# A four-layer graph network, layer 3: split repeat tiles in PSUM, a longer closing pipeline, ten gather sets

## The chip, the cores and the metric

The kernel runs on one core of one Trainium2 chip. The metric is the device time of one execution in microseconds (us); several runs are given by their median. In the profile the engines are PE (TensorE: matmul; PEld is its weight load), DVE (VectorE), ACT (ScalarE), POOL (GpSimd, which here issues the indirect DMAs) and SP (SyncE, which issues plain DMAs).

## The reference

Four layers over 2708 nodes with 128 features. Each is followed by a residual addition and a layer norm. The adjacency matrix is sparse (about 16 neighbours in a row), and the kernel works on lists of neighbours. The change is in the last layer, a graph attention with four heads:

```python
def _gatv2_head(x, A_shape, w1, w2, a, Wlin):
    x1 = x @ w1
    x2 = x @ w2
    E = jax.nn.leaky_relu(x1[:, None, :] + x2[None, :, :], negative_slope=0.01)
    s = E @ a
    s = jnp.tanh(s / 8.0) * 8.0
    s = jnp.exp(s) * A_shape
    s = s / jnp.sum(s, axis=-1, keepdims=True)
    out = s @ x @ Wlin.T
    return jax.nn.leaky_relu(out, negative_slope=0.01)
...
heads = [_gatv2_head(x, A_shape, w1[h], w2[h], a[h], Wlin[h]) for h in range(w1.shape[0])]
return jnp.concatenate(heads, axis=-1) @ w
...
x = _layernorm(x + _L3_gnn_ref(x, adj, ...), axis=-1)
```

## The kernel before

Layer 3 sorts the nodes by their number of neighbours into 24 blocks (`BLOCKS3`, a pair each: neighbour slots g of a node, and quads j of the block, 3 to 8). A chunk is up to 128 edges, one to a partition. Four chunks make a quad; there are 100 quads. `quads` lists them in order, and the loop from L1541 on runs over them.

For each quad the engines do this:

- `fetch` (L1530) takes a tile `g4` of 4 chunks x 644 numbers from the pool `got` and fills it with four indirect DMAs on POOL (L247). A row is x2 of the neighbour for four heads (512), its x (128) and four linear score terms. The pool has `GOT` such sets; a set comes free when the last matmul that reads it is done. `fetch` is called one quad ahead, but POOL runs further ahead as far as sets are free.
- `repeated` (L1350) repeats the block's own x1 over the edges: four matmuls with 32 rows of contraction each (L1358). Three go into the tile `z3` (three PSUM banks), the fourth into `z1`, and a matmul with the identity (L1363) adds the fourth chunk of `g4` to `z1`.
- DVE adds `z3` to the first three chunks (L1555, one instruction over 1536 numbers), scores the fourth out of PSUM (`scores`, L1373, four instructions), and multiplies the relu of the others by the attention vector (`products`, L1381).
- ACT sums these products for each head (`sums_of_products`, L1389: 12 sums in an even quad, 8 in an odd one, where DVE scores the third chunk itself).

Two quads are closed together in `rest` (L1394), a Python generator that hands on at each `yield`. Its stages before: (1) DVE adds the linear terms, L1400 and L1403; (2) ACT tanh and exp, L1405 and L1406; (3) DVE times the adjacency value `val3`, L1409; (4) PE sums over a node's edges, L1414, into `few_ps`; (5) DVE reciprocal `inv` L1419, product L1420, and the mask that spreads the weights into `wm`, L1422; (6) PE multiplies `wm` with x of the neighbours into `po_s`, L1435, which reads the `g4` set for the last time.

When a block's last pair is through, `finish` (L1443) follows: ACT copies `po_s` to `o_ts` (L1448), PE multiplies by Wlin into `pl_s` (L1456), ACT and DVE make the leaky relu `lin_s` (L1461, L1463), PE multiplies by w (L1469 and L1475, into `few_ps`), ACT copies to `y_s` (L1480). After several blocks `normalised3` does the layer norm and scatters the rows out on POOL (L255).

`own_terms` (L1311) prepares the next block while a block's first quads run: a transpose into `few_ps` (L1316), ACT's copy `x_ot` (L1319), x1 and its linear term on PE (L1323 into its own bank, L1324 into `few_ps`), ACT's copy of x1 (L1327) and `al` on DVE (L1330), a matmul into `few_ps` (L1339), and a copy on ACT (L1345).

The order on PE, DVE and ACT is the order in which this Python code calls the instructions. `step` (L1514) advances the generators one stage: the first of `finishing`, then up to two of `closing`, then one of `preparing`. It is called three times in each quad: after the adds and scores (before `repeated` of the next quad), after `products`, and after the sums. I call the three steps of an even quad A, B, C and those of the odd quad behind it D, E, F. A pair's `rest` enters `closing` after its step F, so before the change its six stages fall on A to F of the next pair. A block with an odd number of quads closes its last quad alone, and its `rest` starts in the middle of such a row of steps.

`few_ps` is one PSUM bank, shared by the sums of L1414 (two places), the transpose, the own terms and the output of L1475.

Of the kernel before, what the change touches and what calls it, by code (L numbers as in the profile page):

```python
# [9 lines left out]
FP = mybir.dt.float32  # L10
AF = mybir.ActivationFunctionType
ALU = mybir.AluOpType
# [3 lines left out]
P = 128  # L16
# [5 lines left out]
HEADS = 4  # L22
# [7 lines left out]
HD = HEADS * D  # L30
# [48 lines left out]


TOGETHER3 = [(0, 4), (4, 8), (8, 12), (12, 16), (16, 20), (20, 23), (23, 24)]
GOT = 9


@with_exitstack
def gnn_resnorm_kernel(
# [21 lines left out]
    nc = tc.nc  # L108
# [228 lines left out]
    with ExitStack() as layer:  # L337
        ring = layer.enter_context(tc.tile_pool(name="ring", bufs=RING))
        work = layer.enter_context(tc.tile_pool(name="work", bufs=1))
        small = layer.enter_context(tc.tile_pool(name="small", bufs=2))  # L340
# [692 lines left out]
        ahead = own_row(0)  # L1033
        left = list(range(SPLIT, NBLK))
        for i, b in enumerate(TURNS):
            if i == SPLIT - 2:
                sorted_lists(1)
            x_s, ahead = ahead, own_row(TURNS[i + 1]) if i + 1 < NBLK else None
# [7 lines left out]
            for _ in range(2 if i < 1 else 1):  # L1046
                if left:
                    e = left.pop(0)
# [15 lines left out]
            for _ in range(2 if i in (9, 10, 11) else 1):  # L1064
                if i and again:
                    e = again.pop(0)
# [31 lines left out]
    with ExitStack() as layer:  # L1098
        work = layer.enter_context(tc.tile_pool(name="bn", bufs=1))
        small = layer.enter_context(tc.tile_pool(name="bn_small", bufs=2))  # L1100
# [138 lines left out]
    with ExitStack() as layer:  # L1239
        work = layer.enter_context(tc.tile_pool(name="s3", bufs=1))  # L1240
        mine = layer.enter_context(tc.tile_pool(name="s3_mine", bufs=2))
        got = layer.enter_context(tc.tile_pool(name="s3_got", bufs=GOT))
        small = layer.enter_context(tc.tile_pool(name="s3_small", bufs=3))
        ps_z = layer.enter_context(tc.tile_pool(name="s3_ps_z", bufs=1, space=PSUM))
# [52 lines left out]
        own, closing, finishing, preparing, wide, sums_of = {}, [], [], [], [], {}  # L1297
# [52 lines left out]
        def repeated(b, j, g4):  # L1350

            g, _ = BLOCKS3[b]
            e = g * (P // g)
            z3 = ps_z.tile([P, 3, HD], FP, name="z3")
            z1 = ps_z.tile([P, HD], FP, name="z1")
            for r in range(4):
                rows = slice(32 * r, 32 * r + 32)
                nc.tensor.matmul(  # L1358
                    z3[0:e, r, :] if r < 3 else z1[0:e],
                    lhsT=copies[g][rows, j, :], rhs=own[b][1][rows, :],  # L1360
                    start=True, stop=r < 3, skip_group_check=r == 3,
                )
            nc.tensor.matmul(  # L1363
                z1[0:e], lhsT=ident[0:e, 0:e], rhs=g4[0:e, 3, 0:HD],
                start=False, stop=True, skip_group_check=True,
            )
            return z3, z1

        def scores(e, r, z, a, g4, sc):

# [23 lines left out]
        def rest(b, js, g4s, sc):  # L1394

            g, jj = BLOCKS3[b]
            x_o, _, al = own[b]
            e, k = g * (P // g), 4 * len(js)
            s = sc[0:e, 0:k, :]
            nc.vector.tensor_tensor(s, s, al[0:e, 4 * js[0] : 4 * js[0] + k, :], ALU.add)  # L1400
            for i in range(len(js)):
                s4 = sc[0:e, 4 * i : 4 * i + 4, :]
                nc.vector.tensor_tensor(s4, s4, g4s[i][0:e, :, HD + D : RW], ALU.add)  # L1403
            yield
            nc.scalar.activation(s, s, AF.Tanh, scale=0.125)  # L1405
            nc.scalar.activation(s, s, AF.Exp, scale=8.0)  # L1406
            yield
            c0 = CHUNK3[b] + 4 * js[0]
            nc.vector.tensor_tensor(  # L1409
                s, s, val3[0:e, c0 : c0 + k].unsqueeze(2).to_broadcast((e, k, HEADS)), ALU.mult  # L1410
            )
            yield
            pd = pds[js[0] // 2 % 2]
            nc.tensor.matmul(  # L1414
                pd[0:e, 0:k, :], lhsT=same[g][0:e, :], rhs=s, start=True, stop=True
            )
            yield
            inv = small.tile([P, 8, HEADS], FP, name="inv")
            nc.vector.reciprocal(inv[0:e, 0:k, :], pd[0:e, 0:k, :])  # L1419
            nc.vector.tensor_tensor(s, s, inv[0:e, 0:k, :], ALU.mult)  # L1420
            wm = small.tile([P, 8, g, HEADS], FP, name=f"wm{g}", tag="wm")
            nc.vector.tensor_tensor(  # L1422
                wm[0:e, 0:k],
                mask[g][0:e].unsqueeze(1).unsqueeze(3).to_broadcast((e, k, g, HEADS)),
                s.unsqueeze(2).to_broadcast((e, k, g, HEADS)),
                ALU.mult,
            )
            yield
            if js[0] == 0:
                sums_of[b] = ps_o.tile([P, 512], FP, name="po_s")  # L1430
            po = sums_of[b]
            for i, j in enumerate(js):
                for r in range(4):
                    p0 = 32 * r + j * g
                    nc.tensor.matmul(  # L1435
                        po[:, p0 * HEADS : (p0 + g) * HEADS],
                        lhsT=g4s[i][0:e, r, HD : HD + D], rhs=wm[0:e, 4 * i + r, :, :],
                        start=True, stop=True,
                    )
            if js[-1] == jj - 1:  # L1440
                finishing.append(finish(b, po, x_o))
# [70 lines left out]


        def step(early=True):  # L1514
            for queue, most in ((finishing, 1), (closing, 2), (preparing, 1)):
                if queue is not preparing or early:
                    for work_of in list(queue[:most]):
                        if next(work_of, "done") == "done":
                            queue.remove(work_of)
# [8 lines left out]
        gathered = {}  # L1528
# [9 lines left out]

        fetch(0)
        ahead = repeated(*quads[0], gathered[0])  # L1540
        for i, (b, j) in enumerate(quads):  # L1541
            g, jj = BLOCKS3[b]
            e = g * (P // g)
            if j == 0:
                if b + 1 < NB3:
                    preparing.append(prepare(b + 1))
            if j % 2 == 0:
                sc, g4s = small.tile([P, 8, HEADS], FP, name="sc_s", bufs=4), []
            g4, (z3, z1) = gathered.pop(i), ahead
            g4s.append(g4)  # L1550
            sc4 = sc[:, 4 * (j % 2) : 4 * (j % 2) + 4, :]
            if i + 1 < len(quads):
                fetch(i + 1)
            z = g4[0:e, 0:3, 0:HD]
            nc.vector.tensor_tensor(z, z, z3[0:e], ALU.add)  # L1555
            scores(e, 3, z1, a_99.rearrange("p h d -> p (h d)"), g4, sc4[:, 3, :])
            step()
            if i + 1 < len(quads):
                while quads[i + 1][0] not in own or len(own[quads[i + 1][0]]) < 3:
                    step()  # L1560
                ahead = repeated(*quads[i + 1], gathered[i + 1])
            count = 2 if j % 2 else 3
            products(e, g4, count)
            step()
            sums_of_products(e, g4, sc4, count)
            if count == 2:
                scores(e, 2, g4[:, 2, 0:HD], a_ps, g4, sc4[:, 2, :])
            step()
            if j % 2 or j == jj - 1:
                closing.append(rest(b, list(range(j - j % 2, j + 1)), g4s, sc))  # L1570
# [526 lines left out]
```

## Time and profile before

| | us |
|---|---|
| median of 3 runs | 1935.91 (1930.33 to 1936.26) |
| the profiled execution | 1938.44 |
| its span, first to last instruction | 1936.7 |
| mean granted clock of PE | 0.667 of full speed |
| first and last add L1555 of layer 3 | 1124.99 and 1895.48 |

Busy over the whole span, by engine: PE 1240.9, DVE 1166.6, ACT 776.5, POOL 892.8 us. The groups of layer 3 that matter here, from the list of the costliest groups: busy time, then mean of one in ns.

| line, engine, what | count | us, ns each |
|---|---|---|
| L1358 PE z, four repeats of a quad | 800 | 221.3, 944 (four run side by side) |
| L1363 PE z, identity | 200 | 169.3, 941 |
| L1435 PE po_s | 800 | 128.6, 316 |
| L1555 DVE add of three chunks | 100 | 175.0, 1750 |
| L1381 DVE products | 100 | 151.0, 1510 |
| L1373 DVE scores out of PSUM | 400 | 91.9, 285 |
| L1389 ACT sums | 1024 | 301.3, 296 |
| L247 POOL gather of g | 400 | 398.6, 996 |

A matmul in fp32 appears as two records, so counts on PE are twice those in the code. A row "A <- B: 32.2, 13, 4.0" in the view of waits says that A sat idle 32.2 us in all, 13 times, at most 4.0 us, until B ended; where the releaser is "remote" or "issue", the profile shows none. The releaser is inferred. In the view of windows each engine's busy time is followed by its number of instructions.

### The profile page before, as it was taken

The numbers are of one execution on the slowest core, as the hardware profiler recorded it, in microseconds if no ns is written. First come the engines' busy times: TensorE is split into PE (matmuls) and PEld (weight loads), VectorE is DVE, ScalarE is ACT, GpSimd is POOL, SyncE is SP. The second block draws the span as 40 slices with busy tenths as digits, with TensorE's granted clock in tenths as the row PEclk, the third lists the DMA queues.
The fourth block names the chain that finished last, engine by engine and source line by source line (L and its number), as shares of the span: only waits on it lengthen the run. The fifth ranks groups of instructions, "written<-read, shape, count | busy, mean of one in ns | idle before, by whom it ended". The sixth has DMA issues, their size and how long they took to land. (4 is left out here: it accounts for less than half of the span.)

```text
span 1936.7 us, 23643 instructions
## 1 busy us (share of the span) xinstructions
PE 1240.9 (64%) x5771; PEld 864.1 (45%) x5771; DVE 1166.6 (60%) x4895; ACT 776.5 (40%) x3156; POOL 892.8 (46%) x1003
## 2 busy tenths in 40 slices
PE   7974313353446553554673748888788788878885
PEld 7973212242334442554663314544444444444444
DVE  8997445675635423433447417777678677676774
ACT  3565345543324210211122415555455555445553
POOL 1004654445653366445331474655555556555430
PEclk9986555555555576776676756676676777666675
DMA  8642645666545525223231574865566655756540
GB/s 283 238 150 79 131 140 165 174 183 174 141 103 142 177 43 160 95 92 140 79 113 44 167 239 131 212 190 163 145 196 183 182 166 160 191 150 192 150 115 7
DMA packets 167676, 289.63 MB, mean 150 GB/s; under 512 B 49600, under 2 KB 121502, under 8 KB 160429
## 3 DMA queue, kind: packets, MB, share of 16 engines
q0 software_dynamic: 60496, 190.77, 34.4%
q1 hardware_dynamic: 99489, 92.57, 15.6%
q10 hardware_dynamic: 7544, 4.69, 1.0%
q8 instruction: 48, 0.79, 0.2%
q14 instruction: 99, 0.81, 0.1%
HBM read 242.51 MB, written 45.36 MB: 149 GB/s over the span
## 5 line engine op out<-in xcount | busy, mean ns | idle before, releaser
L247 POOL DMA_INDIRECT g<-t_dram,idx x400 | 398.6, 996 | 316.0 <-issue 178.9
L247 POOL DMA_INDIRECT msg<-d_dram,idx x368 | 348.6, 947 | 260.2 <-issue 164.8
L1389 ACT ACTIVATE sum_junk<-g 126x128 bf16<-126x128 f32 (+3 forms) x1024 | 301.3, 296 | 142.4 <-issue 59.8
L1358 PE MATMUL z<-x,copies 32*126 32x512 f32 (+3 forms) x800 | 221.3, 944 | 65.8 <-DVE g L1555 45.0
L969 PE MATMUL pt_a<-ident,rows 128*128 128x128 f32 (+2 forms) x475 | 114.1, 395 | 144.4 <-ACT at_sb L974 79.5
L1555 DVE TENSOR_TENSOR g<-g,z 126x1536 f32<-126x1536 f32 (+3 forms) x100 | 175.0, 1750 | 44.0 <-DMA g<-t_dram,idx 15.3
L1018 PE MATMUL acc<-x_nat,at_rows 128*128 128x128 f32 (+2 forms) x968 | 160.7, 326 | 52.3 <-DMA at_rows<-at_dram,perm 26.5
L1389 ACT ACTIVATION_READ_ACCUMULATOR sum_junk<-g 126x1 f32 (+3 forms) x1024 | 191.6, 187 | 0.0
L1018 PEld LDWEIGHTS acc<-x_nat,at_rows 128*128 128x128 f32 (+2 forms) x968 | 144.1, 232 | 65.5 <-issue 38.7
L1363 PE MATMUL z<-g,ident 126*126 126x512 f32 (+3 forms) x200 | 169.3, 941 | 0.7 <-issue 0.7
L1435 PE MATMUL po_s<-wm,g 126*128 126x24 f32 (+6 forms) x800 | 128.6, 316 | 58.5 <-DVE wm L1422 56.2
L1435 PEld LDWEIGHTS po_s<-wm,g 126*128 126x128 f32 (+3 forms) x800 | 124.8, 243 | 75.6 <-DVE wm L1422 67.9
L969 PEld LDWEIGHTS pt_a<-ident,rows 128*128 128x128 f32 (+2 forms) x475 | 82.9, 205 | 167.5 <-ACT at_sb L974 92.8
L884 DVE SCALAR_TENSOR_TENSOR own<-msg,ls,own 128x128 f32<-128x128 f32 (+1 forms) x302 | 105.6, 350 | 85.4 <-ACT msg L899 28.5
L1381 DVE SCALAR_TENSOR_TENSOR g<-g,a_ps 126x1536 f32<-126x1536 f32 (+6 forms) x100 | 151.0, 1510 | 0.0
L420 PE MATMUL acc<-x_nat,rows 128*128 128x129 f32 (+3 forms) x1012 | 128.5, 288 | 26.0 <-DMA rows<-in_adj_dram 14.9
L420 PEld LDWEIGHTS acc<-x_nat,rows 128*128 128x128 f32 (+2 forms) x1012 | 123.0, 198 | 31.2 <-DMA rows<-in_adj_dram 16.0
L1358 PEld LDWEIGHTS z<-x,copies 32*126 32x126 f32 (+3 forms) x800 | 67.8, 261 | 100.3 <-issue 46.5
L899 ACT ACTIVATE msg<-msg 128x896 f32<-128x896 f32 (+4 forms) x55 | 50.4, 917 | 132.9 <-DVE msg L896 92.1
L1373 DVE SCALAR_TENSOR_TENSOR g<-z,a 126x128 f32<-126x128 f32 (+3 forms) x400 | 91.9, 285 | 19.5 <-remote 9.2
L445 DVE FIND_INDEX8 ci<-cv,rows 128x8 uint32<-128x247 f32 (+2 forms) x242 | 98.7, 408 | 0.0
L1363 PEld LDWEIGHTS z<-g,ident 126*126 126x126 f32 (+3 forms) x200 | 42.0, 263 | 124.3 <-issue 117.3
(302 smaller groups left out, 2132.2 us busy)
## 6 DMA issues: line engine op xcount, KB each, us to landing
rows<-in_adj_dram SPq DMA_DIRECT2D x34, 1354.0 KB
at_dram<-at_sb SPq DMA_DIRECT2D x105, 256.0 KB
g<-t_dram,idx POOLq DMA_INDIRECT x400
msg<-d_dram,idx POOLq DMA_INDIRECT x368
t_dram<-t_row SPq DMA_DIRECT2D x21, 256.0 KB
x_s<-dx_dram SPq DMA_DIRECT2D x21, 128.0 KB
at_dram<-at_sb SPq DMA_DIRECT2D x21, 64.0 KB
t_dram<-x_nat SPq DMA_DIRECT2D x5, 256.0 KB
```

The costliest lines, as they stand in the source:

```text
L247: nc.gpsimd.indirect_dma_start(out=dst, out_offset=None, in_=table[0:N, :], in_offset=bass.IndirectOffsetOnAxis(ap=index, axis=0),)
L420: nc.tensor.matmul(accs0[k][0:m, c0 : c0 + f1 - f0], lhsT=rows[0:n, j0 : j0 + m], rhs=x_nat[0:n, b, f0:f1], start=k not in started, stop=( ...
L445: nc.vector.max_index(out=ci[0:n, at], in_max=cv[0:n, at], in_values=rows[0:n, c0 : c0 + cw])
L884: nc.vector.scalar_tensor_tensor(to, m, v, last, ALU.mult, ALU.add)
L969: nc.tensor.transpose(pt[0:m, j, 0:n], rows[0:n, c0 : c0 + m], ident[0:n, 0:n])
L1018: nc.tensor.matmul(accs2[ib // 4][0:m, (ib % 4) * D : (ib % 4 + 1) * D], lhsT=at[0:n, i0 : i0 + m], rhs=xw[0:n, b, :], start=(k == 0 and i ...
L1358: nc.tensor.matmul(z3[0:e, r, :] if r < 3 else z1[0:e], lhsT=copies[g][rows, j, :], rhs=own[b][1][rows, :], start=True, stop=r < 3, skip_g ...
L1363: nc.tensor.matmul(z1[0:e], lhsT=ident[0:e, 0:e], rhs=g4[0:e, 3, 0:HD], start=False, stop=True, skip_group_check=True,)
L1381: nc.vector.scalar_tensor_tensor(z, z, 0.0, a_ps[0:e].unsqueeze(1).to_broadcast((e, count, HD)), ALU.max, ALU.mult)
L1389: nc.scalar.activation(junk[0:e], g4[0:e, r, hd * D : (hd + 1) * D], AF.Identity, accum_out=sc[0:e, r, hd : hd + 1],)
L1435: nc.tensor.matmul(po[:, p0 * HEADS : (p0 + g) * HEADS], lhsT=g4s[i][0:e, r, HD : HD + D], rhs=wm[0:e, 4 * i + r, :, :], start=True, stop= ...
L1555: nc.vector.tensor_tensor(z, z, z3[0:e], ALU.add)
```

## The change

The tile `z3` of three banks becomes `z2` (two banks, chunks 0 and 1) and `z0` (one bank, chunk 2); the add L1555 becomes two, over 1024 and over 512 numbers. `rest` gets two more `yield`s: one between the matmul L1414 and `inv`, one between `wm` and the matmul L1435. `inv` to `wm` so come in step F in place of E, and L1435 in step B of the pair after, in place of F; `finish` follows L1435. Up to three of `closing` are advanced in a step in place of two, the score tile `sc_s` has five buffers in place of four, and `GOT` goes from 9 to 10.

```diff
-GOT = 9
+GOT = 10
...
-            z3 = ps_z.tile([P, 3, HD], FP, name="z3")
+            z2 = ps_z.tile([P, 2, HD], FP, name="z2")
+            z0 = ps_z.tile([P, HD], FP, name="z0")
             z1 = ps_z.tile([P, HD], FP, name="z1")
...
-                    z3[0:e, r, :] if r < 3 else z1[0:e],
+                    (z2[0:e, 0], z2[0:e, 1], z0[0:e], z1[0:e])[r],
...
-            return z3, z1
+            return z2, z0, z1
...
                 pd[0:e, 0:k, :], lhsT=same[g][0:e, :], rhs=s, start=True, stop=True
             )
             yield
+            yield
             inv = small.tile([P, 8, HEADS], FP, name="inv")
...
             yield
+            yield
             if js[0] == 0:
                 sums_of[b] = ps_o.tile([P, 512], FP, name="po_s")
...
-            for queue, most in ((finishing, 1), (closing, 2), (preparing, 1)):
+            for queue, most in ((finishing, 1), (closing, 3), (preparing, 1)):
...
-                sc, g4s = small.tile([P, 8, HEADS], FP, name="sc_s", bufs=4), []
-            g4, (z3, z1) = gathered.pop(i), ahead
+                sc, g4s = small.tile([P, 8, HEADS], FP, name="sc_s", bufs=5), []
+            g4, (z2, z0, z1) = gathered.pop(i), ahead
...
-            z = g4[0:e, 0:3, 0:HD]
-            nc.vector.tensor_tensor(z, z, z3[0:e], ALU.add)
+            z = g4[0:e, 0:2, 0:HD]
+            nc.vector.tensor_tensor(z, z, z2[0:e], ALU.add)
+            z = g4[0:e, 2, 0:HD]
+            nc.vector.tensor_tensor(z, z, z0[0:e], ALU.add)
```

## The prediction

> **What bounds the kernel now.** I read the page first. Its chain of waits has four pieces, the last 4 us, so it names nothing for the body. The slices place the work (a digit is a tenth of a slice, busy share; PEclk is the granted clock):
>
> ```profile
> PE   7974313353446553554673748888788788878885
> DVE  8997445675635423433447417777678677676774
> PEclk9986555555555576776676756676676777666675
> ```
>
> Layer 3 fills the slices from the 24th on. Nothing there stands at 9 all along, and the clock is at 6 to 7. The table by stretches has it in us (stretch, length, busy PE, PEld, DVE, ACT, POOL, clock, DMA share, GB/s):
>
> ```profile
> 1400.00:1500.00 100.00, 86.72 (x353) 48.52 (x350) 78.51 (x270) 57.42 (x341) 56.75 (x60) 0.72 0.65 192
> 1600.00:1700.00 100.00, 82.90 (x321) 45.70 (x321) 69.20 (x229) 50.47 (x306) 57.57 (x55) 0.68 0.65 178
> ```
>
> So this is a ring: PE makes z, DVE adds and scores, ACT sums, DVE weights, PE multiplies. A quad takes 7.78 us (the L1555 adds run from 1124.99 to 1895.48, 99 steps). Gathers need 4 x 1.25 = 5.0 us of it, so POOL has room. DVE issues its next instruction at once where it can (L1555 to L1555 in 4.67 us at best), so I ask what DVE waits for. Waits between 1200 and 1880 us (us in total, times, longest):
>
> ```profile
> DVE al L1330 <- PE few_ps L1414: 32.2, 13, 4.0
> DVE inv L1419 <- PE few_ps L1475: 30.6, 13, 4.8
> DVE inv L1419 <- remote: 21.8, 4, 6.7
> DVE sc_s L1409 <- ACT sc_s L1406: 17.1, 7, 6.4
> DVE lin_s L1463 <- ACT lin_s L1461: 10.4, 7, 2.5
> ...
> PE po_s L1435 <- DVE wm L1422: 54.1, 27, 6.8
> PE z L1358 <- DVE g L1555: 35.8, 26, 7.4
> ```
>
> With the smaller rows of the same instructions DVE loses 39.0 us before `al`, 52.4 before `inv`, 30.4 before `lin_s` and 17.1 before the product with val3: 139 us. The two PE rows are what the change aims at, but PE waiting for DVE costs nothing by itself. Note that `inv` needs L1414, yet waits for L1475: both write the one bank `few_ps`. Last, the timeline of PE in one pair of quads:
>
> ```profile
> 1452.92 2.88 PE L1358 MATMUL z<-x,copies 32*128 32x512 f32 x8 [0.47 <-DVE g L1555]
> 1455.73 2.08 PE L1363 MATMUL z<-g,ident 128*128 128x512 f32 x2
> 1457.60 1.80 PE L1323 MATMUL x_ps<-w_s,x_ot 128*128 128x512 f32 x2
> ...
> 1459.38 0.38 PE L1414 MATMUL few_ps<-sc_s,same 126*126 126x32 f32 x2
> 1459.69 1.14 PE L1358 MATMUL z<-x,copies 32*128 32x512 f32 x8
> 1460.76 1.12 PE L1363 MATMUL z<-g,ident 128*128 128x512 f32 x2
> 1461.73 0.33 PE L1339 MATMUL few_ps<-al,alike 128*128 128x64 f32 x2
> 1462.19 1.97 PE L1435 MATMUL po_s<-wm,g 126*128 126x28 f32 x16
> ```
>
> The same two L1363 matmuls take 2.08 us and then 1.12: the clock halves after idle PE and returns in a dense stretch.
>
> **What the Trainium skill says.** "TensorE: Matmul & The Clock Gate", Part 1: the clock runs at half rate until about 3.4 us of sustained activity, and an idle window throttles it again. The trace agrees in kind (2.08 against 1.12), though recovery took some 9 us here. "PSUM — Partial Sum Buffer", PSUM bank collisions: accesses of different engines to one bank and quadrant must be ordered, whatever the columns. The wait of `inv` for L1475 is that. "VectorE: DVE Perf Modes", the errata section: an fp32 tensor_tensor takes (N+151)/0.96 ns; for 1536 that is 1757, the trace has 1750.
>
> **The change, part by part.** [...]"preparing" pairs begin a block (own_terms runs), "finishing" pairs run finish.
>
> *Split of z3.* Each of 100 quads gets one DVE instruction more. By the page 1024 and 512 take 1.224 + 0.691 against 1.757, +0.16; consecutive DVE instructions overlap by 0.08 (1451.02 + 1.75 = 1452.77, next at 1452.69): +0.08. The 1024 and 1536 forms of L1381 (1.203, 1.745) give +0.04. I take 0.06, 5 us in the window. PE may begin z2 0.5 us earlier, but L1363 follows z1, and z1 waits for the scores L1373 as before: worth nothing. If the DMA of the third chunk were late the split could also gain; two gather waits of 15 us in all bound that.
>
> *Closing.* inv and wm move from E to F, po from F to B of the next pair, finish from A-F to C-B. PE's 54 us of waiting for wm go. What is late next:
>
> Finishing pairs, t = 0 at 1463.54: scores end 2.6, z 4.8, L1363 6.8 (1470.32), now po 1.97 to 8.7; ACT's twelve sums end at 8.3, o_ts 0.52 after po to 9.35, L1456 1.89 to 11.3, ACT lin_s 0.54 to 11.95. DVE's odd scores end at 7.75, L1381 and four L1373 (1.13 + 0.84) at 9.75. So `lin_s` waits 2.25 at the low clock; with L1456 at 1.15 (1337.31) and an earlier z it is 0.9. I take 1.9 x 21 blocks = 40 (before: 30.4). `inv` then finds its bank free: L1475 has gone to A of the next pair.
>
> Preparing pairs: `inv` now stands behind L1339, issued in E. After `al` DVE has 1.27 + 0.84 = 2.1 us of work; PE has z, L1363 and L1339, 2.3 us warm (1459.69 to 1462.06), 4.4 cold (1328.55 to 1332.95). Wait 0.2 to 2.2; I take 1.3 x 21 = 27 (before: 52.4). Behind the waiting `inv` DVE has wm and the next quad's two adds queued; PE's z after next, ACT's sums and POOL's next set wait for these in turn, so this wait is on the path in full.
>
> `al`: where the block before has an even number of quads (12 blocks), po now stands ahead of L1323 and L1414. t = 0 at 1451.02: L1363 ends 6.8, po 8.76, L1323 to L1414 2.16 more (less 0.15 of overlap) 10.8, `al` 10.9, while DVE is free at 7.75: 3.1 instead of 1.09. All warm about 1.0. I take 2.1. Where it is odd (10), po leaves that place (at 1322.46 it held L1323 back by 3.6 us) and moves to E: 0.5. Sum 25 + 5 = 30 (before: 39.0).
>
> val3: ACT's exponentials stood behind o_ts, which waited for po (1336.69); that order is gone: 2 (before: 17.1).
>
> Sum: 40 + 27 + 30 + 2 + 5 = 104 against 139, -35 us. DVE is idle 195 us of these 680 (busy 485.02); the other 56 us of waits stay, and some grow when DVE comes earlier to a gather or to sums that ACT has not ended. I keep a quarter back for that: **-26 us**.
>
> *Ten sets, five sc_s.* A set is held two steps (2/3 of a quad) longer and there is one set more: +1/3 quad of lead. POOL has 2.8 us to spare per quad, so nothing; two gather waits of 15 us bound it to -10 to +10. The fifth sc_s and closing 3 only allow the overlap. The out scatters L255 come two steps later in POOL's queue, still between gathers; such a group holds POOL for 14 us as it is (1610.70 to 1624.38), which the lead of about five quads covers; if that lead is gone, the next gather is late by what the group takes. SP's loads of own_x keep their place.
>
> *The end.* Block 22's o_ts comes behind the last twelve sums (+2.7), but the last L1414 no longer stands behind a po of 3.6 us: 0, within 2.
>
> The profiled execution took 1938.4 (span 1936.7 and 1.7 around it); less 26 is 1912. The median of the runs shown is 2.5 lower, so I give **1910**.
>
> **Rivals.** (a) Forecast, 1910, own range 1895 to 1928, chance 0.50. (b) PE, no longer waiting for wm, keeps the high clock: lin_s 19, inv 4, al 12, val3 0, split 4 = 39 us, -100; half of that already meets gather and scatter limits: 1886, chance 0.11. For it: po follows L1363 without a gap; against: PE idles before each even z instead. (c) The moved waits come back elsewhere: 1930 to 1941, chance 0.10. (d) Slower: in preparing pairs po ahead of L1323, then L1339 ahead of `inv`, at the low clock: lin_s 48, inv 46, al 3.1 x 12 + 1.5 x 10 = 52, val3 5, split 7 = 158, +19: 1955. It decides once these waits exceed 139/21 = 6.6 us a block. For it: every L1363 right after idle took 2.07; against: PE's dense stretch is longer now. Chance 0.29. That the change fails to move anything is excluded: the compiled order shows po behind the next quad's z and the two adds.
>
> **Numbers.** A difference of 0.3% (5.8 us) is what can be told from none. Faster 0.61, same 0.10, slower 0.29. The range 1880 to 1952 takes in (a), (b), (c) and the nearer part of (d).
>
> **What would show it.** Right: `po_s <- DVE wm` near 0; `inv` waiting for L1339 (or not at all) and less than 30 us; lin_s waits growing to some 40; the val3 wait gone; L1555's two successors 0.06 us longer together. Wrong: `al` above 50 us, or the mean clock below 0.66, or DVE waiting for gathers for more than 25 us.

## The result and the profile after

The changed kernel takes 1936.87 us (median of 12 runs, 1928.02 to 1952.25). The kernel before took 1931.28 us beside it (12 runs, 1924.35 to 1937.02). The ratio is 1.0035, 95% interval 1.0013 to 1.0058: slower by about a third of a per cent. The forecast was 26 us faster. The profiled execution of the changed kernel took 1937.93 us, its span is 1936.2 us and its mean clock 0.659. In layer 3 the time from the first to the last add of gathered rows went from 770.5 us to 775.3 us (1121.21 to 1896.55).

First the page's slices (a digit is a tenth of a slice), then the view of stretches (length; busy PE, PEld, DVE, ACT, POOL with counts; clock, DMA share, GB/s), both of the changed kernel:

```profile
PE   7974313453546553554774648888887888888875
DVE  8997445675535432433447427677677677677774
PEclk9986555565555666776766756666677676766755
```

```profile
1400.00:1500.00 100.00, 81.08 (x341) 49.40 (x340) 76.28 (x282) 53.19 (x322) 55.54 (x58) 0.74 0.62 185
1600.00:1700.00 100.00, 86.18 (x334) 50.72 (x333) 72.00 (x255) 52.19 (x314) 58.37 (x56) 0.67 0.62 166
```

In the first stretch both engines are a little less busy than in the kernel before, in the second a little busier: the ring as a whole is hardly denser. The waits show why. These are the waits of DVE and then of PE between 1200 and 1880 us in the changed kernel (us in total, times, longest):

```profile
DVE lin_s L1466 <- ACT lin_s L1464: 47.0, 16, 3.8
DVE inv L1421 <- PE few_ps L1339: 35.7, 10, 6.9
DVE sc_s L1410 <- ACT sc_s L1407: 18.3, 10, 3.7
DVE lin_s L1466 <- issue: 13.7, 5, 5.5
```

```profile
PE z L1359 <- DVE g L1558: 37.2, 17, 7.7
PE z L1359 <- issue: 30.6, 11, 6.8
PE pl_s L1459 <- ACT o_ts L1451: 20.9, 20, 2.6
```

The 54.1 us in which PE waited for `wm` are gone, as forecast. DVE gained nothing from it. Its wait for `lin_s` is now 60.7 us (before: 30.4), that for `inv` 43.2 with its smaller rows (before: 52.4), `al` 25.5 (before: 39.0) and val3 18.3 (before: 17.1). That is 147.7 us of waits, where 99 were forecast (104 less the 5 for the split) and 139 stood before; DVE's busy time grew by 7 us (485.02 to 491.90). On the other side the adds waited 25.5 us before and 4.5 us now.

The account closes over the whole layer, from the first add to the last. First the kernel before, then the changed kernel (columns as above; DVE's is the third busy time):

```profile
1124.99:1895.48 770.49, 623.49 (x2424) 351.00 (x2424) 536.36 (x1840) 390.76 (x2332) 412.66 (x414) 0.68 0.60 171
1121.21:1896.55 775.34, 638.04 (x2414) 374.18 (x2414) 543.48 (x1939) 388.43 (x2331) 414.25 (x414) 0.67 0.59 170
```

DVE works 7.1 us longer and stands idle 231.9 us where it stood 234.1. The waits changed places and nearly cancelled, and the layer is 4.8 us longer.

Two places in the timeline of the changed kernel (start, length, engine, line) show the two large rows. First a pair of quads in which a block is finished:

```profile
1439.38 2.07 PE L1364 MATMUL z<-g,ident 126*126 126x512 f32 x2
1441.25 3.45 PE L1438 MATMUL po_s<-wm,g 126*128 126x28 f32 x16
...
1444.74 0.53 ACT L1451 COPY o_ts<-po_s 128x448 f32<-128x448 f32 x1 [1.69 <-PE po_s L1438]
1445.32 2.05 PE L1459 MATMUL pl_s<-o_ts,wlin_s 128*128 128x112 f32 x8 [0.62 <-ACT o_ts L1451]
...
1447.41 0.54 ACT L1464 ACTIVATE lin_s<-pl_s 128x448 f32<-128x448 f32 x1 [2.14 <-issue]
1447.99 0.62 DVE L1466 SCALAR_TENSOR_TENSOR lin_s<-pl_s,lin_s 128x448 f32<-128x448 f32 x1 [3.60 <-ACT lin_s L1464]
```

`po_s`, `o_ts`, `pl_s` and both halves of `lin_s` follow one another without a gap, and DVE stands 3.60 us at the end of that chain. The same sixteen `po_s` records took 1.97 us in the kernel before, with PE warm, that is at its higher rate (L1363 ahead of them took 1.12 us). Then a place where the last quad of an odd block is closed alone while the next block is prepared:

```profile
1370.81 2.07 PE L1364 MATMUL z<-g,ident 126*126 126x512 f32 x2
1372.68 3.45 PE L1438 MATMUL po_s<-wm,g 126*128 126x24 f32 x16
1375.95 0.67 PE L1339 MATMUL few_ps<-al,alike 128*126 128x64 f32 x2
1376.65 0.26 DVE L1421 RECIPROCAL inv<-few_ps 126x16 f32<-126x16 f32 x1 [6.92 <-PE few_ps L1339]
```

`inv` needs the sums of L1415, which were long done. It waits for L1339, because that writes `few_ps` too, the one bank that both share, and L1339 waits behind `po_s` of the pair before. The 16 in its shape (one quad, not two) marks the lone closing. Of the ten waits for L1339 in this window, six are lone closings, and these hold 28.6 of the 35.7 us.

### The profile page after: what moved, and what is told of

The parts are those of the page before. It is cut to its first block, busy times and chain, and to the rows that moved or that the text cites. A ratio compares the mean times of both kernels' runs of the same rounds, so it can differ in the third digit from the quotient of the medians.

```text
span 1936.2 us, 23673 instructions
## 1 busy us (share of the span) xinstructions
PE 1259.7 (65%) x5771; PEld 890.8 (46%) x5771; DVE 1173.3 (61%) x4995; ACT 774.7 (40%) x3156; POOL 894.8 (46%) x1003
## 3 DMA queue, kind: packets, MB, share of 16 engines
q0 software_dynamic: 60496, 190.77, 33.5%
## 4 chain that ended last, share of the span: by engine, by line
PE 34%; DVE 28%; issue 12%; another core or an unknown queue 12%; ACT 7%; DMA 3%; POOL 3%; SPq 0%; DVEq 0%; ACTq 0%; POOLq 0%
PE z L1359 8%; PE z L1364 6%; PE po_s L1438 4%; DVE ci L445 4%; DVE cv L450 3%; ACT sum_junk L1390 3%; PE acc L1018 3%; PE pl_s L1459 2%; POOL msg L247 2%; DVE own L884 2%; DVE msg L896 2%; DVE g L1382 2%; DVE g L1374 2%; DVE k L484 1%
## 5 line engine op out<-in xcount | busy, mean ns | idle before, releaser
L1359 PE MATMUL z<-x,copies 32*126 32x512 f32 (+3 forms) x800 | 239.4, 911 | 96.7 <-issue 53.0
L1364 PE MATMUL z<-g,ident 126*126 126x512 f32 (+3 forms) x200 | 164.4, 916 | 1.1 <-DMA own_x<-x_dram 1.1
L1438 PEld LDWEIGHTS po_s<-wm,g 126*128 126x128 f32 (+3 forms) x800 | 140.1, 261 | 40.8 <-issue 38.3
L1359 PEld LDWEIGHTS z<-x,copies 32*126 32x126 f32 (+3 forms) x800 | 80.1, 250 | 144.3 <-issue 119.4
L420 PEld LDWEIGHTS acc<-x_nat,rows 128*128 128x128 f32 (+2 forms) x1012 | 123.2, 198 | 30.8 <-DMA rows<-in_adj_dram 15.6
L1558 DVE TENSOR_TENSOR g<-g,z 126x1024 f32<-126x1024 f32 (+3 forms) x100 | 121.6, 1216 | 17.8 <-issue 11.4
L1364 PEld LDWEIGHTS z<-g,ident 126*126 126x126 f32 (+3 forms) x200 | 41.2, 258 | 121.8 <-issue 103.0
```

Of the source, the lines that this page charges most:

```text
L420: nc.tensor.matmul(accs0[k][0:m, c0 : c0 + f1 - f0], lhsT=rows[0:n, j0 : j0 + m], rhs=x_nat[0:n, b, f0:f1], start=k not in started, stop=( ...
L1359: nc.tensor.matmul((z2[0:e, 0], z2[0:e, 1], z0[0:e], z1[0:e])[r], lhsT=copies[g][rows, j, :], rhs=own[b][1][rows, :], start=True, stop=r < ...
L1364: nc.tensor.matmul(z1[0:e], lhsT=ident[0:e, 0:e], rhs=g4[0:e, 3, 0:HD], start=False, stop=True, skip_group_check=True,)
L1438: nc.tensor.matmul(po[:, p0 * HEADS : (p0 + g) * HEADS], lhsT=g4s[i][0:e, r, HD : HD + D], rhs=wm[0:e, 4 * i + r, :, :], start=True, stop= ...
```

## The experiments

Eighteen runs were made in five groups, each group beside the kernel before. In the first four groups the kernel before took 1605 to 1609 us, in the last 1916 us, and in the comparison above 1931 us. No run shows what differs between them, so times are compared within a group, and across groups only the ratios to the kernel before. The tables of waits below are for 950 to 1550 us where the kernel before takes some 1607 us. A window holds more quads of a faster kernel, so these rows are not an exact account of the difference.

**Which part of the change costs.** The first group takes the change apart. Only the split:

```diff
-            z3 = ps_z.tile([P, 3, HD], FP, name="z3")
+            z2 = ps_z.tile([P, 2, HD], FP, name="z2")
+            z0 = ps_z.tile([P, HD], FP, name="z0")
...
-            nc.vector.tensor_tensor(z, z, z3[0:e], ALU.add)
+            z = g4[0:e, 0:2, 0:HD]
+            nc.vector.tensor_tensor(z, z, z2[0:e], ALU.add)
+            z = g4[0:e, 2, 0:HD]
+            nc.vector.tensor_tensor(z, z, z0[0:e], ALU.add)
```

> Before, with z3 split into z2 and z0 and nothing else. Theory 1 (the split is pure cost: 100 more DVE instructions of 0.04 to 0.08 us each, two thirds of them on the path): 1.002 to 1.004 of before, DVE busy up by about 7 us. Rival 2 (PE's earlier start on z2 pays): 0.995 or lower, with the wait of PE z for DVE g well below the 35.8 us of before.

Measured: 1610.82 us against 1608.89, ratio 1.0015 (0.9999 to 1.0032). The split costs between nothing and 5 us.

The whole change without the split:

```diff
-GOT = 9
+GOT = 10
...
             yield
+            yield
             inv = small.tile([P, 8, HEADS], FP, name="inv")
...
             yield
+            yield
             if js[0] == 0:
...
-            for queue, most in ((finishing, 1), (closing, 2), (preparing, 1)):
+            for queue, most in ((finishing, 1), (closing, 3), (preparing, 1)):
```

> The changed kernel with z3 left whole (two yields, closing 3, five sc_s, ten sets). Theory 1 (yields only move waits: inv shorter, lin_s longer, val3 unchanged because y_s now stands before tanh): 0.998 to 1.003, DVE wait of lin_s near 60 us, of inv near 43. Rival 2 (the yields gain and the split eats it): 0.993 or lower.

Measured: 1643.1 us, 1.0236 (1.0207 to 1.0265). That is slower than either expectation, though the waits are those named (49.5 us for `lin_s`, 35.5 for `inv`).

The same with nine sets:

```diff
-GOT = 10
+GOT = 9
```

> As the run with the yields, but GOT stays 9. If the tenth set only pays back the longer hold, it is slower than with ten sets by 0.2 to 0.6% and DVE waits for gathers (DMA g) rise above 10 us between 1200 and 1880 us. If the lead of five quads is enough anyway, no difference above 0.2%.

Measured: 1640.4 us, 1.0216 (1.0188 to 1.0244). The tenth set does nothing that can be told. The loss is in the two hand-overs, taken with the third closing and the fifth `sc_s` that go with them.

Only the first hand-over, the one ahead of `inv` (with three closings, five `sc_s` and ten sets):

```diff
             yield
+            yield
             inv = small.tile([P, 8, HEADS], FP, name="inv")
```

> Only the first of the two yields (between the matmul into few_ps and inv), with closing 3, five sc_s and ten sets, z3 whole: inv in F, po in A of the next pair ahead of z, finish from B. Theory 1: lin_s waits less than with both yields (po is a step earlier, 40 us or less), 0.993 to 1.000. Rival: po in A stands ahead of the odd quad's z on PE, so DVE waits for z (L1555 or L1373 behind L1358, L1363) by 1 to 2 us in each of some 45 pairs: 1.01 or higher.

Measured: 1615.89 us, 1.0054 (1.0030 to 1.0078), between the two expectations.

I took the rest, 1.8%, for what the second hand-over costs. That was a mistake, and it stood until the fourth group.

**The shared bank.** The second group has the two kernels again and both with a bank of their own for the denominators. The bank was free only by reading the attention vector from SBUF, where it was copied into PSUM:

```diff
-        ps_a = layer.enter_context(tc.tile_pool(name="s3_ps_a", bufs=1, space=PSUM))
+        ps_d = layer.enter_context(tc.tile_pool(name="s3_ps_d", bufs=1, space=PSUM))
...
-        a_ps = ps_a.tile([P, HD], FP, name="a_ps")
-        nc.vector.tensor_copy(a_ps, a_99.rearrange("p h d -> p (h d)"))
+        a_ps = a_99.rearrange("p h d -> p (h d)")
...
-        pds = [few[:, 32 * i : 32 * i + 32].rearrange("p (k h) -> p k h", h=HEADS) for i in (0, 1)]
+        dens = ps_d.tile([P, 512], FP, name="dens_ps")
+        pds = [dens[:, 32 * i : 32 * i + 32].rearrange("p (k h) -> p k h", h=HEADS) for i in (0, 1)]
```

The changed kernel as it is:

> The changed kernel itself once more, since the yields alone gave 1.024 where before took 1609 us, and the whole change 1.0035 where it took 1931 us. Theory 1 (waits without a named releaser, about 1 us behind a hand-over, are long where before takes 1931 us; the longer distance between hand-overs hides them there and only costs where they are absent): on a chip where before takes near 1610 us, 1.02 to 1.03; where it takes near 1930 us, 1.001 to 1.006. Rival (the split of z3 gives back what the yields cost): 1.000 to 1.006 on either.

Measured: 1648.37 us, 1.0242 (1.0210 to 1.0273).

The kernel before, one execution for its trace:

> Before once more, for its profile beside the others of this call. On a chip where it takes near 1610 us: DVE waits in layer 3 almost all with a named releaser, al near 38 us, inv near 20, lin_s near 26, val3 near 0.

Measured: 1604.28 us.

The changed kernel with the bank:

> The changed kernel with the sums of the matmul before inv in a bank of their own (the copy of the attention vector in PSUM gives its bank up; DVE reads it from SBUF). Theory 1 (inv waits for L1339 only because they share a bank): the waits of inv on the own terms' matmul and of al on the sums' matmul vanish, 0.970 to 0.985 of the changed kernel. Rival (PE is what is late, not the bank): DVE waits as long elsewhere, within 0.5% of the changed kernel. If L1381 becomes slower with two SBUF inputs (over 1.80 us for 1536), this has to be taken off.

Measured: 1609.69 us, 1.0023 (0.9999 to 1.0048). Against the kernel before as it stands, nearly all of the loss is gone.

The kernel before with the bank:

> Before with the same bank of its own for the sums. Theory 1: inv no longer waits for L1475 (20 to 50 us), al no longer for L1414 (32 to 38 us): 0.965 to 0.985 of before. Rival: within 0.5% of before.

Measured: 1596.77 us, 0.9927 (0.9903 to 0.9951): faster than both kernels, by less than the theory had. So the bank helps the kernel before as well. Like for like, with the bank in both, the change still costs about 1 per cent (1.0023 over 0.9927), where it costs 2.4 without. The waits of DVE, first in the kernel before, then in the changed kernel of this group:

```profile
DVE al L1330 <- PE few_ps L1414: 34.6, 18, 3.8
DVE lin_s L1463 <- ACT lin_s L1461: 25.8, 19, 1.6
DVE inv L1419 <- PE few_ps L1475: 19.4, 15, 3.6
```

```profile
DVE lin_s L1466 <- ACT lin_s L1464: 49.7, 20, 3.7
DVE inv L1421 <- PE few_ps L1339: 36.8, 11, 5.9
DVE al L1330 <- PE few_ps L1415: 15.5, 10, 4.1
```

`inv` waits for L1475 before and for L1339 after. With the bank neither row is left (the trace of both kernels with the bank has no row of `inv`), while `lin_s` stays at 48.9 in the changed kernel and 27.5 in the kernel before. The layer from first to last add: 651.3 us before, 691.2 changed; with the bank 642.6 and 661.4. The change adds 39.9 us without the bank and 18.8 with it, so about half of the loss goes with the shared bank. With the bank, DVE is busy 8.7 us longer in the changed kernel (533.26 to 541.97 over the layer), which has the split, and waits 21 us more for `lin_s`; part of that comes back at other rows.

**One hand-over more in front of `lin_s`.** The third group asks whether the remaining wait is a cost of its own:

```diff
             nc.scalar.activation(lin[:, :, 0:n], pl[:, :, 0:n], AF.Copy, scale=0.01)
             yield
+            yield
```

The changed kernel with this:

> The changed kernel with one more hand-over in `finish`, between ScalarE's scaling of lin_s and VectorE's maximum over it; nothing is left out of the computation. Theory: in the changed kernel po_s, o_ts, pl_s and lin_s follow one another inside a single pair of blocks, and VectorE waits 50 us in layer 3 for lin_s on a chip where the kernel before takes about 1607 us; a later lin_s leaves less than 15 us of that, the wait for the reciprocal behind few_ps (37 us) stays, and the time falls from about 1646 us by 15 to 35 us. Rival, that the reciprocal's wait alone counts: the 30 us come back as a longer wait for the reciprocal or for the products and the time stays within 5 us of 1646.

Measured: 1667.04 us, 1.0411 (1.0351 to 1.0470). Theory and rival were both wrong: it is slower than the changed kernel in the other groups. The wait for `lin_s` is gone from the trace, and `inv` now waits 35.0 us behind L1415 besides 22.6 behind L1339.

The changed kernel with the attention vector in SBUF but the denominators still in `few_ps`, that is, the bank's edit without the bank:

```diff
-        ps_a = layer.enter_context(tc.tile_pool(name="s3_ps_a", bufs=1, space=PSUM))
...
-        a_ps = ps_a.tile([P, HD], FP, name="a_ps")
-        nc.vector.tensor_copy(a_ps, a_99.rearrange("p h d -> p (h d)"))
+        a_ps = a_99.rearrange("p h d -> p (h d)")
```

> The changed kernel with the own values read from SBUF in place of a_ps in PSUM, but with the denominators still in few_ps: the other half of the kernel with a bank of its own for them. Nothing of the computation is left out. Theory (the shared bank is what costs): no gain, 1646 us or up to 15 us more, since the gathers of line 247 become about 170 ns longer each and the wait for the reciprocal behind few_ps stays at 30 us or more. Rival (that kernel was faster because a_ps was gone): about 1610 us as there.

Measured: 1650.82 us, 1.0299 (1.0252 to 1.0346), with 36.7 us of `inv` behind the shared bank as before. So it was the denominators' own place that helped. They got a tile of their own in a bank of their own; no run separates the one from the other.

The changed kernel with the bank and the later `lin_s`:

> The changed kernel with both edits: denominators in a bank of their own, and lin_s one hand-over later. Nothing is left out. Theory (two causes, in series on VectorE): the bank alone gave 1610 us with 49 us of waiting for lin_s left, so this gives 1575 to 1600 us. Rival (VectorE is then held by the gathers or by TensorE as a whole, each hand-over only moves waits): 1605 to 1620 us.

Measured: 1631.63 us, 1.0177 (1.0130 to 1.0225), worse than with the bank alone and than both expectations. The waits of DVE there say why:

```profile
DVE inv L1421 <- PE dens_ps L1415: 34.3, 17, 3.4
DVE al L1330 <- PE few_ps L1324: 27.1, 12, 4.5
DVE al L1330 <- PE few_ps L1479: 20.7, 4, 6.6
```

The wait for `lin_s` is gone, but L1415 stands behind `pl_s` in PE's queue, and `pl_s` waits for `o_ts` (21.8 us, 18 times). `inv` now waits for that same chain. `lin_s` had only been the first to meet it.

The kernel before with both edits:

> The kernel before with both edits. Nothing is left out. Theory: the bank alone gave 1597 us with 27.5 us of waiting for lin_s left, so 1575 to 1592 us, and it is level with the changed kernel that has both edits or ahead of it by the split's 2 to 3 us. Rival: within 4 us of 1597 us, the wait turns up at the adds of the gathered rows (17 and 14 us there).

Measured: 1581.46 us, 0.9869 (0.9816 to 0.9922). With the bank alone it was 0.9927, in another group and with an interval that overlaps; the repeat below lies clear of that. So the edit that costs in the changed kernel does no harm here and seems a small gain. That points to which instructions then share a step, rather than to how many hand-overs there are.

**The second hand-over alone.** The fourth group was made to settle that.

The changed kernel once more:

> The changed kernel again, beside the kernel before, as a measure for the three others of this group. If the loss belongs to the instruction order alone, the ratio is near 1.024, as in the last group with this kernel; if the kernel before takes some 1930 us here, as in the first comparison, the ratio is near 1.0035.

Measured: 1645.96 us, 1.0255 (1.0225 to 1.0284).

Only the second hand-over (with the same three closings, five `sc_s` and ten sets):

```diff
             yield
+            yield
             if js[0] == 0:
                 sums_of[b] = ps_o.tile([P, 512], FP, name="po_s")
```

> The kernel before with only the second new hand-over, the one between wm and the weighted sums (three closings at once, five sc_s, ten sets; the reciprocal where it was, the gathered rows added three repeats at once). Nothing is left out. Theory (the second hand-over costs by itself, because po_s, o_ts, pl_s and lin_s then share one pair of blocks and po_s stands ahead of own_terms on TensorE): ratio 1.012 to 1.022, VectorE's waits for lin_s at 45 us or more from 950 to 1550 us where the kernel before takes about 1607 us. Rival (it costs only together with the first, through the reciprocal behind few_ps): ratio 1.000 to 1.006.

Measured: 1563.32 us, 0.9732 (0.9697 to 0.9766). My theory and its rival both fall. Alone the second hand-over is worth 43 us, more than anything else tried in that group. Its waits, and below them those of the kernel with only the first (its lines stand one lower, so L1476 is L1475 of the kernel before):

```profile
DVE al L1330 <- PE few_ps L1414: 28.1, 13, 6.8
...
DVE inv L1419 <- PE few_ps L1414: 4.4, 2, 3.1
...
DVE lin_s L1464 <- ACT lin_s L1462: 3.2, 11, 0.4
```

```profile
DVE inv L1420 <- PE few_ps L1476: 39.4, 19, 4.8
DVE inv L1420 <- PE few_ps L1339: 15.6, 12, 2.4
DVE al L1330 <- PE few_ps L1414: 12.8, 9, 2.9
...
DVE lin_s L1464 <- ACT lin_s L1462: 2.9, 9, 1.0
```

Each hand-over alone moves `po_s` by one step and with it the whole of `finish`; both end the wait for `lin_s` (2.9 and 3.2 us). They differ in `inv` alone. In steps (a dash marks the pair after; within a step `finish` comes first, then `rest`, then `own_terms`; L1339 is in E):

| | inv | po_s | DVE lin_s | output matmuls (L1475) | ratio |
|---|---|---|---|---|---|
| before | E | F | D | E | 1 |
| second only | E | A' | E | F | 0.9732 |
| first only | F | A' | E | F | 1.0054 |
| both | F | B' | F | A' | 1.0236 |

In the kernel before, `inv` stands behind the output matmuls, which write `few_ps` ahead of it in the same step E. The second hand-over moves these to F and leaves `inv` in E, ahead of them and of L1339. The first moves `inv` after them into F, and behind L1339 as well. Both together take the output matmuls away again but leave `inv` behind L1339, put `po_s` in front of L1339 where a block has an odd number of quads, and bring `lin_s` to the end of an unbroken chain.

How the chain is spread with the second hand-over alone (timeline of that kernel; columns as above):

```profile
1249.53 0.59 ACT L1449 COPY o_ts<-po_s 128x512 f32<-128x512 f32 x1 [0.32 <-PE po_s L1436]
1253.62 1.92 PE L1457 MATMUL pl_s<-o_ts,wlin_s 128*128 128x128 f32 x8
...
1256.42 0.57 ACT L1462 ACTIVATE lin_s<-pl_s 128x512 f32<-128x512 f32 x1
1258.52 0.68 DVE L1464 SCALAR_TENSOR_TENSOR lin_s<-pl_s,lin_s 128x512 f32<-128x512 f32 x1
1259.12 0.35 DVE L1419 RECIPROCAL inv<-few_ps 126x32 f32<-126x32 f32 x1
...
1260.14 1.06 PE L1476 MATMUL few_ps<-wout_s,lin_s 128*128 128x128 f32 x8
```

The chain takes 9 us from `o_ts` to `lin_s` instead of 3.3, with other work in every gap, and `inv` reads the bank just before L1476 writes it.

The changed kernel with the bank, once more:

> The changed kernel with the denominators in a bank of their own, once more, to have it beside the changed kernel and the second hand-over in one comparison. Theory: the bank takes back at least three quarters of the changed kernel's loss in this group. Rival (where the kernel before takes some 1930 us, the waits are of another kind): it takes back less than a third.

Measured: 1608.70 us, 1.0028 (1.0012 to 1.0045), 45.0 us of waiting for `lin_s`. Against the kernel before without the bank, 2.3 of the 2.55 per cent are gone, as in the second group.

The kernel before with the bank and the later `lin_s`, once more:

> The kernel before with the bank and the later lin_s, once more. Theory: 0.980 to 0.992 of the kernel before, and the fastest of the four. Rival (its gain in the last group was one group's luck, since its interval was 1 percent wide): 0.992 or more.

Measured: 1583.30 us, 0.9861 (0.9832 to 0.9890). It holds up, but is not the fastest. Its edit to `finish` moves the output matmuls from E to F, as the second hand-over does.

**Each single hand-over with the bank.** If the first one is dear only because `few_ps` holds `inv`, a bank of its own must make the two alike. The edits are those shown: one hand-over each, and the bank.

> The kernel with only the second hand-over, and the denominators in a bank of their own. Nothing is left out. With the shared bank it took 0.973 of the kernel before; left there are 28 us in which VectorE waits for al behind the denominators' matmul in few_ps, and none to speak of for the reciprocal. Theory (the bank pays only where the reciprocal or al stands behind it): 0.962 to 0.972. Rival (with the longer gathers the bank is a loss once the reciprocal does not wait): 0.973 or more.

Measured: 1854.83 us against 1915.68, 0.9659 (0.9615 to 0.9703), as the theory had it.

> The kernel with only the first hand-over, and the denominators in a bank of their own. Nothing is left out. The first and the second hand-over alone put the weighted sums at the same place and differ in the reciprocal's alone; they took 1.005 and 0.973 of the kernel before. Theory (what makes the later reciprocal dear is that few_ps holds it behind the matmuls of line 1476 and line 1339, 55 us there): its waits fall below 10 us and the ratio is 0.970 to 0.988. Rival (the reciprocal is then too late for wm and the weighted sums by itself, TensorE waits 45 us for wm there): 0.998 or more.

Measured: 1845.76 us, 0.9614 (0.9569 to 0.9660), faster than the theory had and far from the rival. The two are alike within their intervals, where they had been 3.2 per cent apart. This comparison is across groups, since this group ran where the kernel before takes 1916 us, and neither single hand-over was tried there without the bank. The waits bear it out. From 1200 to 1800 us, the kernel with the first hand-over and the bank, PE's row added below:

```profile
DVE inv L1420 <- remote: 7.8, 1, 7.8
...
DVE inv L1420 <- PE dens_ps L1414: 1.2, 1, 1.2
...
DVE inv L1420 <- PE few_ps L1339: 1.2, 1, 1.2
```

```profile
PE po_s L1436 <- DVE wm L1423: 25.5, 15, 7.9
```

The reciprocal waits 10.2 us in all, against 55.0 us with the shared bank (39.4 + 15.6). PE still waits 25.5 us for `wm`, against 7.9 with the second hand-over and the bank, and that shows in no time. Both kernels are faster than the kernel before of their group, and no run of the changed kernel was that. Without the bank, the second hand-over alone is faster than both, in the group where all three ran.

The bank does not make two hand-overs as good as one. With it, and with the split, they read 1.0023 and 1.0028, although `inv` hardly waits there; the second alone reads 0.9732 even without the bank. What is left between these two is mainly the wait for `lin_s`, 48.9 and 45.0 us against 3.2. That this wait is the cause is argued from the traces: the two runs that removed it from the changed kernel got other waits in its place.

## Why the prediction was wrong

**What held.** The view of waits named the right places. `po_s <- DVE wm` vanished. `inv` moved from L1475 to L1339. The split was forecast at 5 us and DVE is 7 us busier; alone it cost 1.9 us, with an interval that takes in both nothing and 5. `al` was forecast at 30 and measured 25.5. The ten sets were put at nothing, and the runs with nine and ten agree. That PE's wait for `wm` costs nothing by itself fits the runs: the changed kernel has no such row and takes 1648 us, while the kernel before waits 25.7 us and takes 1607; and with the bank 25.5 us against 7.9 made no difference between the single hand-overs. (Without the bank the first has 45.1 us and the second 1.1, and there the slower one is the one that waits, so that pair alone would not show it.)

**What failed first: `inv` in preparing pairs.** The step was "Wait 0.2 to 2.2; I take 1.3 x 21 = 27", against 43.2 measured. It was worked out for blocks with an even number of quads. For those the trace agrees: 2.09, 1.46, 1.11 and 2.42 us. For the odd ones the text said that `po_s` "leaves that place" and "moves to E: 0.5", and priced only what this does to `al`. In E `po_s` stands directly ahead of L1339, and the lone closing's `inv` stands behind L1339: 1.8 to 6.9 us each, six times, 28.6 us. The move was seen and its place was right; what stood behind the new place was not followed. Where the kernel before takes 1607 us the same can be compared: nine lone closings of the changed kernel wait 33.5 us for L1339, and with the first hand-over alone, which leaves `po_s` a step earlier, eight wait 12.2 us, none over 2.5. That ties the long ones to `po_s`.

**What failed second: the size of `lin_s`.** The step was "now po 1.97 to 8.7", and 1.9 us a block, 40 in all; measured 60.7, of which 13.7 have no named releaser. The chain was right link by link. Its first link was taken at 1.97 us, from a row behind an L1363 of 1.12 us. In all eleven blocks from 1200 to 1880 us with an even number of quads `po_s` took 3.43 to 3.46 us, behind an L1364 of 2.07. The 2.25 us "at the low clock" become 3.73 when these 1.48 us are added, and eight of the eleven waited 3.6 to 3.7 (36.6 of the 60.7 us stand in these eleven blocks); the milder mean of 1.9 counted on pairs at the high rate, of which there were none. "TensorE: Matmul & The Clock Gate" of the Trainium skill, Part 1, has the two rates; the prediction cited it, and then took a matmul at the full rate for a place where the trace shows the half rate. Two of its readings of the rate were also loose. The recovery that it put at some 9 us is nearer 7 in its own lines (1452.92 to 1459.69). And "every L1363 right after idle took 2.07" holds for 31 of the 33 whose L1358 had waited 0.4 us or more; the other two took 1.12 and 1.62.

**What failed third: val3.** The step was "that order is gone: 2", measured 18.3. `o_ts` no longer stands ahead of ACT's tanh and exponentials, but `y_s` does, in step B, and it waits for PE: ahead of each of the ten waits for val3, ACT stood 4.8 to 6.9 us before `y_s`, with tanh right behind it. The waits of ACT from 1200 to 1880 us in the changed kernel:

```profile
ACT y_s L1483 <- PE z L1364: 30.6, 6, 5.8
...
ACT y_s L1483 <- PE po_s L1438: 23.5, 4, 6.9
```

The instruction that left the queue was counted, the one that took its place was not. This row was not tested by a run of its own. Where the kernel before takes 1607 us, it is absent in the changed kernel, although `y_s` waits there too (20.6 us behind L1316, at most 3.3), so the order alone does not make it.

The three terms missed by 16, 21 and 16 us, and `al` by 4.5 the other way: the 49 us by which the waits exceed the 99 forecast. The miss in time is smaller, some 32 us (26 faster forecast, 5.6 slower measured), because the adds then waited 21 us less, a gain that no term of the sum had. The rival on the slower side had the mechanism ("L1339 ahead of `inv`, at the low clock", `inv` 46, `lin_s` 48). Its sum of 158 us is close to the 147.7 of waits and 7 of busy time that were measured, in part by luck, since `al` was 27 us too long in it and `lin_s` and val3 13 too short each. Its 1955 was too slow because it, too, had no gain at the adds.

**What is shown and what stays open.** Shown, where the kernel before takes 1607 us: the hand-overs carry the loss, not the split or the sets; about half of it goes with the shared bank; the second hand-over alone is a gain and the first alone is not, and with the bank, in the slower group, the two are alike, so what shares a bank with `inv` in its step is the difference. Argued from traces only: that the rest of the loss is the chain in front of `lin_s`. Open: why the same change costs 2.4 per cent there and 0.35 where it was first measured. In that first trace DVE's idle time without a named releaser is 82.1 us of the layer in the kernel before and 60.6 in the changed one; in the other two it is 0.9 and nothing. The changed kernel's waits may cover part of such hold-ups; no run separates this. Nor was any part of the change tried without the bank in that state, so the 0.35 per cent themselves were not taken apart.

The page of the Trainium skill that the prediction named, "PSUM — Partial Sum Buffer", PSUM bank collisions raise a hardware error, fits the result: accesses of two engines to one bank and quadrant (32 partitions) must be ordered, whatever their columns. The waits of `inv` agree: 19.4 us behind L1475, 36.8 behind L1339, and neither row with a bank apart.

## What to carry to other kernels

When an instruction moves to a later step, list what it is now ahead of as well as what it was ahead of, for each kind of block and not only the common one, and follow every bank that these instructions share. When a remedy helps the changed kernel, try it in the kernel before as well: here the bank helped both, and only half of the loss was its own. A hand-over is worth what its new neighbours make of it: try each alone before both together, because the cost of the pair minus the cost of one said nothing about the other (1.8 per cent slower by subtraction, 2.7 per cent faster when measured). Take a matmul's duration from a row with the same clock as the place where it will stand.

## What the runs showed of the hardware

Reading the attention vector from SBUF made POOL's gathers longer. The group of costliest instructions for the kernel before, and for the changed kernel with that edit alone (count, busy us, mean ns, idle time before it):

```profile
L247 POOL DMA_INDIRECT g<-t_dram,idx x400 | 398.8, 997 | 196.2 <-issue 115.0 <-ACT y_s L1480 23.8 <-ACT sum_junk L1389 22.3
```

```profile
L247 POOL DMA_INDIRECT g<-t_dram,idx x400 | 459.3, 1148 | 187.3 <-issue 89.7 <-ACT sum_junk L1388 67.4 <-DMA own_x<-x_dram 8.2
```

The DVE products kept their 1.51 us on average (1511 and 1516 ns in the kernel before without and with the bank), while a gather went from 997 to between 1136 and 1177 ns in all kernels with the edit. "SBUF — State Buffer" of the Trainium skill, Who interferes with whom, says that a DVE instruction with two SBUF inputs contends with a GpSimd instruction that reads SBUF; the gathers read their index lists there, so the trace agrees in direction; which of the two held the other no run shows. It cost about 60 us of POOL's time and little of the kernel's: with it and no other gain the changed kernel read 1.0299, against 1.0255 and 1.0242 for the changed kernel in other groups.

The kernel before took 1931 us in one group, some 1607 in four and 1916 in the last; the changed kernel 1937 us in the first and 1646 to 1648 us in two of the four. The instructions in the traces last equally long (a gather 996 and 997 ns, an add of 1536 numbers 1750 ns in both), so the difference lies in the gaps: in layer 3 DVE stands idle 234.1 us in the slower trace and 117.6 in the faster, 82.1 and 0.9 of it without a named releaser. What sets it is not shown.
